# Keys and values of two groups by seven products in one bank; the value bias moved behind the context

## The chip, the cores and the metric

The kernel runs on one core of a Trainium2 chip. The metric is the device time of one launch in microseconds (us). An executed kernel has five engines beside its DMA queues: PE multiplies matrices into PSUM, the accumulators, which come in banks; DVE, ACT and POOL do the elementwise work (POOL on SBUF alone); SP issues most of the DMAs. PEld is PE's weight load, which runs beside its matmuls.

## The reference

One transformer layer in fp32, x of shape (2, 512, 512): grouped attention with 32 query heads and 8 key-value groups of width 128, then a layer norm, then a linear layer with low-rank experts and a router, then a layer norm. What matters here is the attention:

```
q = hidden_states @ Wq + bq
k = hidden_states @ Wk + bk
v = hidden_states @ Wv + bv
...
q = _rope(q, pos)
k = _rope(k, pos)
...
probs = jax.nn.softmax(scores, axis=-1)
ctx = jnp.einsum('bgrst,bgtd->bgrsd', probs, v)
...
return ctx @ Wo + bo
```

Causal scores are masked before the softmax, so each row of probs sums to one.

## The kernel before

**Units.** The work is cut into 16 units, one for each pair of group and batch row; the last two groups are taken with the batch outside. A unit has 16 slots, numbered through all units by T (256 in all, some 2.9 us each in the middle). One slot scores 32 query positions of four heads against the keys so far (`score`, L488), takes the masked maximum on DVE (L496), the exponential on ACT (L503), a reciprocal (L507), the normalisation on ACT (L511) and block transposes on DVE (L519, L521), each of these one or more slots behind. Four slots make a part; the probabilities go through DRAM to be transposed (L529, L537), and `weigh` (L544) multiplies them by the values twelve slots behind. `context_out` (L550) copies the result to SBUF on ACT.

**The order** is written out by hand: `slot(T)` issues in a fixed sequence what each engine does in that slot, and `put(T, f)` adds single steps (loads, sums of weights) to the end of a slot. Each engine takes its instructions in that order. What is issued for PE stands at the head of the slot: a product of queries, a product of keys or values, a product of the output, the score, the contexts.

**Seven products.** Queries and the output projection are multiplied as two-by-two block matrices by seven block products instead of eight. The sums of blocks of x are made once (`x_sums`), the sums of weight blocks on POOL (`strassen_sums`, L416 to L419), and the products of a pair of heads run through two PSUM tiles, qx and qy, in the order of `q_products` (two matmuls of 256 columns each, L429). Three times the running sum in qx is copied to small tiles by ACT and once to its place (`q_copy`, L457 and L460), and DVE adds qy to the three small ones (`q_sum`, L467, L470, L472).

**Keys** are made plainly, one unit ahead: four matmuls of 512 columns in slots 0 to 3 of a unit (`k_mm`, L355, tile pp, one PSUM bank that has the tag "k"), then the rotation in three steps on DVE from PSUM (L368, L371, L375) and a sum on POOL (L376).

**Values** are made plainly too, for two groups at a time: for a tile of 128 tokens, four matmuls of 256 columns with x as the weights (`v_mm`, L342, tile pv). In the middle of the kernel a unit makes two such tiles, in slots 7, 8, 11 and 12, in the same bank "k". DVE adds the bias, which is broadcast over all partitions by a DMA, and writes them to SBUF (`v_out`, L347), into one of eleven tiles. The first pair's eight tiles and three of the second pair's are made before or early in the slots, in other banks.

**Experts.** `lora_weights` transposes gathered rows on PE in three steps at slots 12, 14 and 16: the rows of the low-rank factors (L283), the router's rows (L289), and the other factors (L295). The bank tag is "wx".

Of the kernel before, what the change touches and what calls it, by code (L numbers as in the profile page):

```python
# [15 lines left out]
P = 128  # L16
H = 32
# [12 lines left out]
def postln_layer_kernel(  # L30
# [85 lines left out]
    bqkT = const.tile([P, H + G], F32, name="bqkT")  # L116
# [44 lines left out]
    def load_wv(gg):  # L161
        wv_g = wts.tile([P, KC, VN], F32, tag="wv_g", name=f"wv_{gg}", bufs=1)
        nc.sync.dma_start(out=wv_g, in_=Wv[:, ts(gg, VN)].rearrange("(c p) n -> p c n", p=P))
        bv_g = wts.tile([P, VN], F32, tag="bv_g", name=f"bv_{gg}")
        nc.sync.dma_start(out=bv_g, in_=bv[ts(gg, VN)].partition_broadcast(P))
        wvs[gg] = wv_g, bv_g
# [22 lines left out]
    bqk = setup.tile([H + G, D], F32, name="bqk")  # L189
    nc.scalar.dma_start(out=bqk[:H, :], in_=bq.rearrange("(h d) -> h d", d=D))  # L190
    nc.scalar.dma_start(out=bqk[H:, :], in_=bk.rearrange("(h d) -> h d", d=D))
# [27 lines left out]
    a_act = setup.tile([EAR, HID], F32, name="a_act")  # L219
    r_act = setup.tile([EA, HID], F32, name="r_act")  # L220
# [42 lines left out]
    def gather_experts():  # L263
        gather(a_act, lora_A.rearrange("e r n -> (e r) n"), idx["a"])
        gather(r_act, router_W, idx["e"])
# [72 lines left out]
    def v_mm(gg, t, c, pool, tag):  # L338

        if c == 0:  # L340
            psq["v", gg, t] = pool.tile([P, VN], F32, tag=tag, name="pv")
        nc.tensor.matmul(  # L342
            psq["v", gg, t], lhsT=xT[:, c, ts(t, P)], rhs=wvs[gg][0][:, c, :], start=(c == 0), stop=(c == KC - 1))
# [14 lines left out]
    def rope_step(key, bias_col, part, dst):  # L358
# [14 lines left out]
        else:  # L373
# [3 lines left out]
                dst, t1[:].rearrange("p (n s) -> p n s", s=BLK), t2[:].rearrange("p (n s) -> p n s", s=BLK), ALU.add)  # L377
# [76 lines left out]

    def q_copy(u, k, name):
        if name == "c21":
            nc.scalar.copy(psq["q", u, 2 * k + 1][:, :TH], halves[u, k]["qx"])  # L457
            return
        part = halves[u, k][name] = proj.tile([P, TH], F32, tag=name, name=name)
        nc.scalar.copy(part, halves[u, k]["qx"])  # L460

    def q_sum(u, k, step):
        key = u, k
        z = halves[key]
        if step == 0:
            psq["q", u, 2 * k] = proj.tile([P, S], F32, tag="raw0", name="q0", bufs=2)
            nc.vector.tensor_tensor(psq["q", u, 2 * k][:, :TH], z["qy"], z["p1"], ALU.add)  # L467
        elif step == 2:
            psq["q", u, 2 * k + 1] = proj.tile([P, S], F32, tag="raw1", name="q1")
            nc.vector.tensor_tensor(psq["q", u, 2 * k + 1][:, TH:], z["qy"], z["u3"], ALU.add)  # L470
        else:
            nc.vector.tensor_tensor(psq["q", u, 2 * k][:, TH:], z["qy"], z["u2"], ALU.add)  # L472
# [66 lines left out]
    def weigh(p, j):  # L539
        u, i = parts[p]  # L540
        g, b = unit(u)
        if j == 0:
            psc[p] = ps_ctx.tile([P, R, P], F32, tag="ctx", name="pc")
        nc.tensor.matmul(  # L544
            psc[p], lhsT=v_sb[g // VG, b * TPB + j][:, ts(g % VG, D)], rhs=pT[p][:, :, ts(j, P)],
# [591 lines left out]
```

## Time and profile before

| | |
|---|---|
| median of 4 runs | 841.21 us (840.48 to 846.49) |
| the profiled execution | 840.93 us |
| its span, first to last instruction | 839.1 us |
| mean granted clock of PE | 0.996 |
| weight loads and matmuls recorded | 3201 of each |
| key matmuls of 512 columns (L355, from wk) | 128 records |
| value matmuls of 256 columns (L342) | 256 records |
| value results with bias on DVE (L347) | 32, mean 410 ns |
| context copies on ACT (L550) | 64, mean 586 ns |
| value bias loads by SP | 4 of 128 KB, 6.7 us to landing |

The profile is of one execution. A group of instructions is named by its line, engine and operation, then "out<-in" by the program's tile names, then shapes, then the number of records; behind the bar stand busy time in us, the mean of one in ns, and the idle time of the engine before them with what ended it. Matmuls overlap, so the mean duration of one is longer than the distance from its start to the next; the modelled ends make a busy PE look fuller than it is. The start times of the timeline have no such trouble.

### The profile page before, as it was taken

How to read it: one execution, taken by the hardware profiler on the slowest of the kernel's cores; microseconds unless marked ns; L12 is line 12 of the kernel's file. 1: busy time of each engine (PE TensorE's matmuls, PEld its weight loads, DVE VectorE, ACT ScalarE, POOL GpSimd, SP SyncE). 2: the span in 40 equal slices, each digit the busy share in tenths (PEclk: the TensorE clock that was granted, in tenths of full speed). 3: DMA queues.
4: the chain of work that ended last, by engine and by line, in shares of the span. 5: the costliest groups of instructions: out<-in, count | busy, mean ns of one | idle time of the engine just before them, and what ended most of it. 6: DMA issues, size and time to landing. Idle time of an engine off the chain costs nothing.

```text
span 839.1 us, 10734 instructions
## 1 busy us (share of the span) xinstructions
PE 826.4 (98%) x3201; PEld 584.4 (70%) x3201; DVE 595.4 (71%) x1963; ACT 353.0 (42%) x1000; POOL 292.4 (35%) x319
## 2 busy tenths in 40 slices
PE   9999999999999999999999999999999999999996
PEld 5567767677777777777777777777777776555564
DVE  4468977787767876786867866787767968853534
ACT  1225454544435344434435344434434444662132
POOL 6463344233332334233332334344333523300023
PEclk9999999999999999999999999999999999999998
DMA  9126536463653556362653556273644545674211
GB/s 292 35 64 194 152 96 183 110 186 103 157 155 101 163 165 170 79 189 85 154 152 102 163 165 174 71 220 111 152 135 130 164 113 187 171 231 113 62 39 62
DMA packets 84971, 116.47 MB, mean 139 GB/s; under 512 B 6581, under 2 KB 64797, under 8 KB 82866
## 3 DMA queue, kind: packets, MB, share of 16 engines
q1 hardware_dynamic: 84258, 115.50, 48.4%
q0 software_dynamic: 448, 0.14, 0.2%
q8 instruction: 25, 0.41, 0.2%
q14 instruction: 32, 0.26, 0.1%
q10 hardware_dynamic: 208, 0.15, 0.1%
HBM read 71.73 MB, written 44.04 MB: 138 GB/s over the span
## 4 chain that ended last, share of the span: by engine, by line
PE 93%; DVE 4%; DMA 1%; ACT 1%; POOL 1%; issue 1%; SPq 0%; DVEq 0%; POOLq 0%
PE pc L544 16%; PE sc L488 13%; PE qx L429 11%; PE wx L429 11%; PE pp L355 10%; PE qy L429 8%; PE wy L429 8%; PE pv L342 7%; PE py L679 3%; PE po L615 3%; PE tp L274 1%; PE py L724 1%; DMA pT<-db 1%; DMA db<-zt 0%; DVE wt L568 0%
## 5 line engine op out<-in xcount | busy, mean ns | idle before, releaser
L503 ACT ACTIVATE p<-sc,nmax 128x288 f32<-128x288 f32 (+15 forms) x256 | 124.4, 486 | 253.1 <-DVE nmax L496 207.6
L496 DVE CUSTOM_DVE_ANT_0 sc<-sc,maskw 128x288 f32<-128x288 f32 (+15 forms) x256 | 114.2, 446 | 154.3 <-PE sc L488 151.6
L544 PE MATMUL pc<-pT,v 128*128 128x512 f32 x320 | 165.5, 599 | 0.4 <-DMA pT<-db 0.4
L488 PE MATMUL sc<-kT,qT 128*128 128x160 f32 (+15 forms) x512 | 162.0, 398 | 1.1 <-ACT p L503 1.1
L376 POOL TENSOR_TENSOR qT<-q,t 128x512 f32<-128x512 f32 x56 | 71.2, 1271 | 187.9 <-DVE q L375 187.9
L511 ACT ACTIVATE p<-p,den 128x288 f32<-128x288 f32 (+15 forms) x256 | 133.4, 522 | 0.1
L488 PEld LDWEIGHTS sc<-kT,qT 128*128 128x128 f32 x512 | 96.7, 190 | 30.3 <-issue 14.3
L416 POOL TENSOR_TENSOR cs<-ctxT 128x256 f32<-128x256 f32 x28 | 26.5, 947 | 196.1 <-PE wy L429 109.4
L550 ACT COPY ctxT<-pc 128x512 f32<-128x512 f32 x64 | 37.5, 586 | 124.0 <-PE pc L544 124.0
L519 DVE STREAM_TRANSPOSE zt<-p 128x128 f32<-128x128 f32 (+2 forms) x192 | 81.7, 426 | 0.0
L544 PEld LDWEIGHTS pc<-pT,v 128*128 128x128 f32 x320 | 57.0, 190 | 19.5 <-issue 5.4
L355 PE MATMUL pp<-xT,wk 128*128 128x512 f32 x128 | 65.0, 593 | 0.5 <-ACT xT L275 0.5
L342 PE MATMUL pv<-wv,xT 128*128 128x256 f32 x256 | 63.6, 379 | 0.0
L429 PE MATMUL wx<-wo,ctxT 128*128 128x256 f32 x224 | 57.7, 380 | 0.4 <-DVE den L507 0.4
L429 PE MATMUL qx<-xs,wq 128*128 128x256 f32 x224 | 58.0, 381 | 0.0
L342 PEld LDWEIGHTS pv<-wv,xT 128*128 128x128 f32 x256 | 48.5, 190 | 13.4 <-issue 6.9
L521 DVE STREAM_TRANSPOSE zt<-p 128x32 f32<-128x32 f32 (+3 forms) x256 | 57.5, 225 | 0.0
L429 PEld LDWEIGHTS qx<-xs,wq 128*128 128x128 f32 x224 | 41.4, 190 | 22.3 <-issue 16.0
L429 PEld LDWEIGHTS wx<-wo,ctxT 128*128 128x128 f32 x224 | 42.4, 190 | 13.5 <-issue 7.6
L503 ACT ACTIVATION_READ_ACCUMULATOR p<-sc,nmax 128x1 f32 x256 | 49.9, 195 | 0.0
L601 DVE TENSOR_TENSOR x_sb<-wx,x_sb 128x256 f32<-128x256 f32 x112 | 47.0, 419 | 0.0
L368 DVE SCALAR_TENSOR_TENSOR t<-q,bqkT,rope_sb 64x512 f32<-64x512 f32 x56 | 43.0, 768 | 1.3
(187 smaller groups left out, 1365.2 us busy)
## 6 DMA issues: line engine op xcount, KB each, us to landing
db<-zt SPq DMA_DIRECT2D x64, 256.0 KB, 4.2
pT<-db SPq DMA_DIRECT2D x16, 1024.0 KB, 4.8
db<-zt SPq DMA_DIRECT2D x64, 192.0 KB, 3.3
pT<-db SPq DMA_DIRECT2D x16, 768.0 KB, 4.4
wq<-in_L_attn_Wq_dram SPq DMA_DIRECT2D x20, 512.0 KB, 4.8
wo<-in_L_attn_Wo_dram SPq DMA_DIRECT2D x10, 1024.0 KB, 7.6
db<-zt SPq DMA_DIRECT2D x64, 128.0 KB, 2.4
pT<-db SPq DMA_DIRECT2D x16, 512.0 KB, 4.2
```

What stands on the lines that cost most here:

```text
L342: nc.tensor.matmul(psq["v", gg, t], lhsT=xT[:, c, ts(t, P)], rhs=wvs[gg][0][:, c, :], start=(c == 0), stop=(c == KC - 1))
L355: nc.tensor.matmul(psq[key], lhsT=wt[:, c, cols], rhs=xT[:, c, ts(b, S)], start=(c == 0), stop=(c == KC - 1))
L376: nc.gpsimd.tensor_tensor(dst, t1[:].rearrange("p (n s) -> p n s", s=BLK), t2[:].rearrange("p (n s) -> p n s", s=BLK), ALU.add)
L429: nc.tensor.matmul(ps, lhsT=wt[:, c, :], rhs=xt[:, c, :], start=start and c == 0, stop=c == CH - 1, skip_group_check=True)
L488: nc.tensor.matmul(sc[s][:, :w], lhsT=qT[u][:, i * QB + n].rearrange("p r s -> p (r s)"), rhs=kT[u][:].rearrange("p n s -> p (n s)")[:, :w ...
L496: nc.vector.tensor_tensor_reduce(sc[s][:, :w], sc[s][:, :w], maskw[:, S - w :], -SCALE, -MASKED, ALU.add, ALU.min, nmax[s])
L503: nc.scalar.activation(ptile[s][:, :w], sc[s][:, :w], AF.Exp, bias=nmax[s], scale=-1.0, accum_out=rden[s])
L511: nc.scalar.activation(ptile[s][:, :w], ptile[s][:, :w], AF.Copy, scale=rden[s])
L519: nc.vector.transpose(z[:, :, last - i : last, n, :].rearrange("p q j s -> p j q s"), ptile[s][:, : i * P])
L521: nc.vector.transpose(z[:, : n + 1, last, n, :], ptile[s][:, i * P : w])
L544: nc.tensor.matmul(psc[p], lhsT=v_sb[g // VG, b * TPB + j][:, ts(g % VG, D)], rhs=pT[p][:, :, ts(j, P)], start=(j == 0), stop=(j == i))
L601: nc.vector.tensor_tensor(into, pw[k, bank], into, ALU.add)
```

## The change

Units 0 to 3 keep their plain keys; the first pair of groups and half of the second keep plain values (pair 1's batch row 0, now four tiles). For all others, keys and values are made by seven block products for two groups and one batch row at a time: such a block takes a stretch of 16 slots, starting at slot 7 of a unit, with a product on every second slot and a result between them. Six blocks of keys and five of values fill the stretches one after another.

Both running sums of a block lie in the two halves of one bank. Four results a block are copied by ACT to the place in SBUF where the result belongs, and three are added there by DVE to what waits in that place. For keys the two blocks of columns are the two groups and the output is a unit's key tile, which is then rotated in place (key tiles: five instead of two). For values the weights of PE are blocks of x of 128 tokens, and the output has 128 columns.

The sums of weight blocks are made on POOL by the function that the queries use, six sets in all. The value bias is not added to the values: since the probabilities of a row sum to one, it is added to the context, by the instruction that copies it (now an activation with a bias of one column). It is loaded and transposed with the biases of queries and keys, and its four broadcast loads go. Plain value results become copies on ACT. The queries' partial results wait in the place of their result too, which takes away three small tiles. The router's rows are gathered into the tile of the low-rank rows and transposed with them. Loads of keys and values have other slots.

```
+    NBIAS = H + 2 * G
+    bqkT = const.tile([P, NBIAS], F32, name="bqkT")
...
-        bv_g = wts.tile([P, VN], F32, tag="bv_g", name=f"bv_{gg}")
-        nc.sync.dma_start(out=bv_g, in_=bv[ts(gg, VN)].partition_broadcast(P))
-        wvs[gg] = wv_g, bv_g
+        wvs[gg] = wv_g
...
-    bqk = setup.tile([H + G, D], F32, name="bqk")
+    bqk = setup.tile([NBIAS, D], F32, name="bqk")
     nc.scalar.dma_start(out=bqk[:H, :], in_=bq.rearrange("(h d) -> h d", d=D))
-    nc.scalar.dma_start(out=bqk[H:, :], in_=bk.rearrange("(h d) -> h d", d=D))
+    nc.scalar.dma_start(out=bqk[H : H + G, :], in_=bk.rearrange("(h d) -> h d", d=D))
+    nc.scalar.dma_start(out=bqk[H + G :, :], in_=bv.rearrange("(h d) -> h d", d=D))
     for t in range(TPB):
         load_x(t, 1)
...
-    a_act = setup.tile([EAR, HID], F32, name="a_act")
-    r_act = setup.tile([EA, HID], F32, name="r_act")
+    ar_act = setup.tile([EAR + EA, HID], F32, name="ar_act")
...
-        gather(a_act, lora_A.rearrange("e r n -> (e r) n"), idx["a"])
-        gather(r_act, router_W, idx["e"])
+        gather(ar_act[:EAR, :], lora_A.rearrange("e r n -> (e r) n"), idx["a"])
+        gather(ar_act[EAR:, :], router_W, idx["e"])
         for a in range(EA):
             gather(b_act[:, a, :], lora_B.rearrange("e (p j) r -> (e p) (j r)", j=BJ), idx["b"][:, a : a + 1])
...
-            ta = ps_wo.tile([P, KC, EAR], F32, tag="wx", name="ta")
+            ta = ps_wo.tile([P, KC, EAR + EA], F32, tag="wx", name="ta")
             for c in range(KC):
-                nc.tensor.transpose(ta[:, c, :], a_act[:, ts(c, P)], ident[:EAR, :EAR])
-            nc.vector.tensor_copy(arT[:, :, :EAR], ta)
+                nc.tensor.transpose(ta[:, c, :], ar_act[:, ts(c, P)], ident[: EAR + EA, : EAR + EA])
+            nc.vector.tensor_copy(arT, ta)
             nc.vector.tensor_copy(b_jar, b_act.rearrange("p a (j r) -> p j a r", r=RK))
-        elif step == 1:
-            tr = ps_wo.tile([P, KC, EA], F32, tag="wx", name="tr")
-            for c in range(KC):
-                nc.tensor.transpose(tr[:, c, :], r_act[:, ts(c, P)], ident[:EA, :EA])
-            nc.vector.tensor_copy(arT[:, :, EAR:], tr)
         else:
...
-            psq["v", gg, t], lhsT=xT[:, c, ts(t, P)], rhs=wvs[gg][0][:, c, :], start=(c == 0), stop=(c == KC - 1))
+            psq["v", gg, t], lhsT=xT[:, c, ts(t, P)], rhs=wvs[gg][:, c, :], start=(c == 0), stop=(c == KC - 1))
+    def v_of(gg, b):
+        if (gg, b) not in v_sb:
+            v_sb[gg, b] = work.tile([P, TPB, VN], F32, tag="v", name=f"v_{gg}_{b}", bufs=3)
+        return v_sb[gg, b]
     def v_out(gg, t):
-        v_sb[gg, t] = work.tile([P, VN], F32, tag="v", name=f"v_{gg}_{t}", bufs=11)
-        nc.vector.tensor_tensor(v_sb[gg, t], psq["v", gg, t], wvs[gg][1], ALU.add)
+        nc.scalar.copy(v_of(gg, t // TPB)[:, t % TPB, :], psq["v", gg, t])
     in_psum = set()
...
+    def k_of(u):
+        if u not in kT:
+            kT[u] = work.tile([P, UNIT, BLK], F32, tag="kT", name=f"kT_{u}", bufs=5)
+        return kT[u]
     def k_rope(u, part):
         if part == 0:
-            kT[u] = work.tile([P, UNIT, BLK], F32, tag="kT", name=f"kT_{u}")
+            k_of(u)
         rope_step(("k", u), H + unit(u)[0], part, kT[u])
...
+    def q_half(u, k, name):
+        head, half = {"p1": (0, 0), "u2": (0, 1), "c21": (1, 0), "u3": (1, 1)}[name]
+        return psq["q", u, 2 * k + head][:, half * TH : (half + 1) * TH]
     def q_copy(u, k, name):
-        if name == "c21":
-            nc.scalar.copy(psq["q", u, 2 * k + 1][:, :TH], halves[u, k]["qx"])
-            return
-        part = halves[u, k][name] = proj.tile([P, TH], F32, tag=name, name=name)
-        nc.scalar.copy(part, halves[u, k]["qx"])
-    def q_sum(u, k, step):
-        key = u, k
-        z = halves[key]
-        if step == 0:
+        if name == "p1":
             psq["q", u, 2 * k] = proj.tile([P, S], F32, tag="raw0", name="q0", bufs=2)
-            nc.vector.tensor_tensor(psq["q", u, 2 * k][:, :TH], z["qy"], z["p1"], ALU.add)
-        elif step == 2:
+        elif name == "u3":
             psq["q", u, 2 * k + 1] = proj.tile([P, S], F32, tag="raw1", name="q1")
-            nc.vector.tensor_tensor(psq["q", u, 2 * k + 1][:, TH:], z["qy"], z["u3"], ALU.add)
+        nc.scalar.copy(q_half(u, k, name), halves[u, k]["qx"])
+    def q_sum(u, k, name):
+        into = q_half(u, k, name)
+        nc.vector.tensor_tensor(into, halves[u, k]["qy"], into, ALU.add)
+    kvs = {}
+    KV_STEPS = {0: 1, 2: 2, 4: 6, 6: 7, 8: 4, 10: 5, 12: 3}
+    KV_OUT = {1: "p1", 3: "c11", 5: "u2", 7: "u3", 9: "c21", 11: "c22", 13: "c12"}
...
+    KV_ON_ACT = ("p1", "u2", "u3", "c21")
+    def kv_block(kind, p, h, c):
+        if kind == "k":
+            return wqk["k", VG * p + h][:, CH * c : CH * (c + 1), :]
+        return wvs[p][:, CH * c : CH * (c + 1), ts(h, D)]
+    def kv_sums(kind, p):
+        w = kvs[kind, p] = late["pool"].tile([P, 3, CH, D], F32, tag="kvs", name=f"kvs_{kind}_{p}")
+        strassen_sums(
+            nc.gpsimd, *(kv_block(kind, p, h, c) for h in range(2) for c in range(2)), *(w[:, m] for m in range(3)))
+    def kv_products(kind, p, b, step):
+        key = kind, p, b
+        x1, x2 = (xT[:, CH * c : CH * (c + 1), ts(b, S)] for c in range(2))
+        if step == 1:
+            halves[key] = ps_k.tile([P, 2, TH], F32, tag="k", name=f"{kind}x")
+        half, w, xt = {
+            1: (0, (0, 0), x1[:, :, :TH]), 2: (1, (0, 1), x2[:, :, :TH]), 6: (0, 1, xs[:, b, 1]),
+            7: (0, (1, 0), xs[:, b, 2]), 4: (0, (1, 1), xs[:, b, 3]), 5: (1, 0, xs[:, b, 0]),
+            3: (1, 2, x2[:, :, TH:]),
+        }[step]
+        w = kv_block(kind, p, *w) if isinstance(w, tuple) else kvs[kind, p][:, w]
+        ps = halves[key][:, half]
+        first = step in (1, 5)
+        if kind == "k":
+            product(ps, w, xt, first)
         else:
-            nc.vector.tensor_tensor(psq["q", u, 2 * k][:, TH:], z["qy"], z["u2"], ALU.add)
+            for t in range(2):
+                for c in range(CH):
+                    nc.tensor.matmul(
+                        ps[:, ts(t, P)], lhsT=xt[:, c, ts(t, P)], rhs=w[:, c, :],
+                        start=first and t == c == 0, stop=c == CH - 1, skip_group_check=True)
+    def kv_out(kind, p, b, name):
+        h, half = {
+            "p1": (0, 0), "c11": (0, 0), "u2": (0, 1), "c12": (0, 1), "c21": (1, 0), "u3": (1, 1), "c22": (1, 1)}[name]
+        x, y = (halves[kind, p, b][:, n] for n in range(2))
+        if kind == "k":
+            u = units.index((VG * p + h, b))
+            into = k_of(u)[:, half * (UNIT // 2) : (half + 1) * (UNIT // 2), :].rearrange("p n s -> p (n s)")
+            psq["k", u] = kT[u][:].rearrange("p n s -> p (n s)")
+        else:
+            into = v_of(p, b)[:, 2 * half : 2 * half + 2, ts(h, D)]
+            x, y = (z.rearrange("p (t d) -> p t d", d=D) for z in (x, y))
+        if name in KV_ON_ACT:
+            nc.scalar.copy(into, x)
+        else:
+            nc.vector.tensor_tensor(into, y, into, ALU.add)
     def q_rope(u, r, part):
         if u not in qT:
...
     def context_out(p):
         ctxT[p] = work.tile([P, R, P], F32, tag="ctxT", name=f"ctxT_{p}", bufs=3)
-        nc.scalar.copy(ctxT[p], psc[p])
+        col = H + G + unit(parts[p][0])[0]
+        nc.scalar.activation(ctxT[p], psc[p], AF.Identity, bias=bqkT[:, col : col + 1])
...
-    for n, gg, t in [(2 * t - 1, 0, TPB + t) for t in range(TPB)] + [(2 * t + 11, 1, t) for t in range(3)]:
+    for n, gg, t in [(2 * t - 1, 0, TPB + t) for t in range(TPB)] + [(2 * t + 11, 1, t) for t in range(TPB)]:
         put(n, lambda gg=gg, t=t: v_tile(gg, t, ps_wo, "wx"))
...
-        put(12 + 2 * k, lambda k=k: lora_weights(k))
+        if k < 2:
+            put(12 + 4 * k, lambda k=k: lora_weights(k))
     put(1, lambda: load_q(1, 1))
     put(6, lambda: load_wv(1))
...
-        put(2 * UNIT * (g - 1) - 24, lambda g=g: load_k(g))
-    for gg in range(2, G // VG):
-        put(4 * UNIT * (gg - 1) + 30, lambda gg=gg: load_wv(gg))
+    PLAIN_K = 2 * B
+    KV_FROM = 7
+    late = {}
+    PERIOD = VG * B * UNIT
+    for p in range(1, G // VG):
+        at = PERIOD * p
+        put(8 if p == 1 else at - PERIOD + 8, lambda p=p: load_k(VG * p))
+        put(36 if p == 1 else at - PERIOD + 10, lambda p=p: load_k(VG * p + 1))
+        put(40 if p == 1 else at - 2 * UNIT + 3, lambda p=p: kv_sums("k", p))
+        if p > 1:
+            put(at - PERIOD + 34, lambda p=p: load_wv(p))
+        put(at + (UNIT if p == 1 else 0) + 3, lambda p=p: kv_sums("v", p))
+    def kv_at(T):
+        frame, o = divmod(T - KV_FROM, UNIT)
+        p, k = divmod(frame + B, VG * B)
+        kind, b = "kv"[k // B], k % B
+        if 0 < p < G // VG and (kind, p, b) != ("v", 1, 0):
+            return (kind, p, b), o
+        return None, None
     def wo_from(u):
...
-        if 0 < uk < NU and l < KC:
+        if 0 < uk < PLAIN_K and l < KC:
             k_mm(uk, l)
-        gv, tv = divmod(2 * (uk - 3) + (l >= 11), NT)
-        gv += 1
-        new_v = 0 < gv < G // VG and (gv > 1 or tv >= 3)
-        if new_v and l in (7, 8, 11, 12):
-            for c in range(2):
-                v_mm(gv, tv, 2 * (l in (8, 12)) + c, ps_k, "k")
+        kv, o = kv_at(T)
+        if kv and o in KV_STEPS:
+            kv_products(*kv, KV_STEPS[o])
         kw, sw = divmod(T - LAG_WO, 8)
...
+        if kv and KV_OUT.get(o) in KV_ON_ACT:
+            kv_out(*kv, KV_OUT[o])
         for part, j in weigh_at.get(T - 1, ()):
...
-            q_sum(uq, kq, {1: 0, 5: 2, 7: 3}[step])
+            q_sum(uq, kq, {1: "p1", 5: "u3", 7: "u2"}[step])
+        if kv and o in KV_OUT and KV_OUT[o] not in KV_ON_ACT:
+            kv_out(*kv, KV_OUT[o])
         if 0 <= T - 2 < T_END:
             reciprocals(T - 2)
         if 0 <= T - 4 < T_END:
...
-        if new_v and l in (10, 14):
-            v_out(gv, tv)
         if plain and step_o:
             wo_out(p)
...
-    tb = ps_sc.tile([P, H + G], F32, tag="sc", name="tb")
-    nc.tensor.transpose(tb, bqk, ident[: H + G, : H + G])
+    tb = ps_sc.tile([P, NBIAS], F32, tag="sc", name="tb")
+    nc.tensor.transpose(tb, bqk, ident[:NBIAS, :NBIAS])
     nc.vector.tensor_copy(bqkT, tb)
     for c in range(KC):
...
+    late["pool"] = proj_stack.enter_context(tc.tile_pool(name="late", bufs=1))
     T_PROJ = T_END - 19
```

More of the change, by code (lines that the diff above doesn't have):

```diff
@@ L115, in postln_layer_kernel @@
     rope_sb = const.tile([P, 2, S], F32, name="rope_sb")
-    bqkT = const.tile([P, H + G], F32, name="bqkT")
+    NBIAS = H + 2 * G
+    bqkT = const.tile([P, NBIAS], F32, name="bqkT")
     OH, ARH = O // 2, EAR // 2
@@ L376, in rope_step @@
             nc.gpsimd.tensor_tensor(
-                dst, t1[:].rearrange("p (n s) -> p n s", s=BLK), t2[:].rearrange("p (n s) -> p n s", s=BLK), ALU.add)
+                dst, t1[:, :].rearrange("p (n s) -> p n s", s=BLK), t2[:, :].rearrange("p (n s) -> p n s", s=BLK), ALU.add)
     def k_mm(u, c):
@@ L544, in weigh @@
         nc.tensor.matmul(
-            psc[p], lhsT=v_sb[g // VG, b * TPB + j][:, ts(g % VG, D)], rhs=pT[p][:, :, ts(j, P)],
+            psc[p], lhsT=v_sb[g // VG, b][:, j, ts(g % VG, D)], rhs=pT[p][:, :, ts(j, P)],
             start=(j == 0), stop=(j == i))
@@ L807, in postln_layer_kernel @@
             put(q_from(set_units(before)[-1], k_before) + 8, lambda n=n, k=k: load_q(n, k))
-    for g in range(2, G):
-        put(2 * UNIT * (g - 1) - 24, lambda g=g: load_k(g))
-    for gg in range(2, G // VG):
-        put(4 * UNIT * (gg - 1) + 30, lambda gg=gg: load_wv(gg))
+    PLAIN_K = 2 * B
[17 more added lines that the diff above has]
+        return None, None
     def wo_from(u):
```

## The prediction

> **What bounds the kernel now.** I read first the totals at the head of the page (engine, busy us, share of the span, instructions):
>
> ```profile
> span 839.1 us, 10734 instructions
> ...
> PE 826.4 (98%) x3201; PEld 584.4 (70%) x3201; DVE 595.4 (71%) x1963; ACT 353.0 (42%) x1000; POOL 292.4 (35%) x319
> ...
> PE 93%; DVE 4%; DMA 1%; ACT 1%; POOL 1%; issue 1%; SPq 0%; DVEq 0%; POOLq 0%
> ```
>
> PE is busy for all but 12.7 us, and the chain that ended last (second line) is PE for 93%. The busy time by stretches says where the 12.7 us lie: 1.9 in the first 50 us, 0.3 from 50 to 100, none from 100 to 700, the rest in the tail. So in the long middle, where nearly all of the change lies, time is the sum of what PE streams. As PE's ends are modelled, I price by starts, from PE's timeline (start, length, operation, records merged):
>
> ```profile
> 11.54 7.03 PE L355 MATMUL pp<-xT,wq 128*128 128x512 f32 x16
> 18.41 1.89 PE L342 MATMUL pv<-wv,xT 128*128 128x256 f32 x8
> ...
> 29.21 5.34 PE L342 MATMUL pv<-wv,xT 128*128 128x256 f32 x24
> 34.39 6.17 PE L355 MATMUL pp<-xT,wq 128*128 128x512 f32 x14
> ```
>
> 16 records of 512 columns take 18.41 - 11.54 = 6.87 us, 0.4294 each; 24 of 256 take 5.18, 0.2158 each. A matmul of the program is two records, each with a weight load of its own. The same view later in the span has short ones:
>
> ```profile
> 308.91 0.30 PE L488 MATMUL sc<-kT,qT 128*128 128x32 f32 x2
> 309.05 1.10 PE L544 MATMUL pc<-pT,v 128*128 128x512 f32 x2
> 309.99 1.03 PE L429 MATMUL qx<-xs,ws 128*128 128x256 f32 x4
> ...
> 318.18 0.38 PE L488 MATMUL sc<-kT,qT 128*128 128x128 f32 x2
> 318.40 1.03 PE L429 MATMUL wy<-wo,cs 128*128 128x256 f32 x4
> ```
>
> Two records of 128 columns take 0.22 us, 0.110 each. Two of 32 and two of 512 take 309.99 - 308.91 = 1.08 us, of which the long two are 0.86: a record of 32 holds PE for 0.11, not the 0.027 of its columns. That is the weight load showing. At 128 columns load and stream just balance.
>
> **PE's work, part by part.** The groups by line and shape say how much there is:
>
> ```profile
> L355 PE MATMUL pp<-xT,wk 128*128 128x512 f32 x128 | 65.0, 593 | 0.5 <-ACT xT L275 0.5
> L342 PE MATMUL pv<-wv,xT 128*128 128x256 f32 x256 | 63.6, 379 | 0.0
> ```
>
> *Keys.* 128 records are 16 units of 4 matmuls. Units 0 to 3 stay; 12 units leave: 96 records x 0.4294 = 41.2 us. In come six (pair, batch) blocks of seven products, each two matmuls of 256 columns, so 28 records: 168 x 0.2158 = 36.3. **-5.0 us**.
>
> *Values.* 256 records are 32 tiles of 4 matmuls; 12 tiles stay (eight of pair 0, four of pair 1), 20 leave: 160 x 0.2158 = 34.5 us. In come five blocks of seven products, but with x as weights and 128 columns of output: four matmuls each, 56 records a block, 280 in all. At 0.110 that is 30.8: **-3.7 us**. Here one eighth of the arithmetic goes, yet the records rise from 160 to 280, each with a weight load: this is the step that could turn. Its price lies between 0.108 (half of 0.2158) and 0.190, the duration of one such load; I take 0.110, because the 128-column score is the same shape and type and its two loads are in that spacing.
>
> The Trainium skill speaks against this step ("TensorE: Matmul & The Clock Gate", Back-to-back issue gap): in a stream of load and matmul pairs it gives 81 ns a matmul of 128 columns against 56 for one alone. An estimate by that page's ratio, 1.45, makes 0.159 of my 0.110, and the values 10 us dearer instead of 3.7 cheaper. The trace's 0.22 us for two, loads included, decides for me.
>
> *Router.* Its four transposes (L289, 4 records, 0.4 us) become four more rows of L283's: **-0.3**, between 0 and -0.4.
>
> Sum: -9.0 us.
>
> **What lies beside PE.** ACT: 12 plain value copies and 44 of the blocks, 56 x 0.367 (L457, same shape) = 20.6; the bias makes L550 an activation, 0.687 (the 512-wide exponential, which reads a bias too) for 0.586, x64 = 6.5. ACT goes from 353 to 380 of 830. DVE: -32 x 0.41 (L347), +33 x 0.415 (L467's form): +0.6 of 595. POOL: six sums of four instructions, 0.731 + 0.907 + 0.763 + 0.753 = 3.15 us a set (rows of L416 to L419): +18.9 of 292. All three are hidden by PE's 817 us; uncovered they would matter only as lateness within a slot, which I follow for each queue:
>
> ACT. Behind a block's copy stand context copy, normalisation and exponential of that slot, and score needs the exponential of two slots before. Copies come on slots 8, 12, 14 and 0 of 16 and delay these by 0.37. The narrowest place is the 64-wide score (ACT's timeline):
>
> ```profile
> 313.91 0.59 ACT L550 COPY ctxT<-pc 128x512 f32<-128x512 f32 x1 [2.49 <-PE pc L544]
> ...
> 315.02 0.30 ACT L503 ACTIVATE p<-sc,nmax 128x64 f32<-128x64 f32 x1
> 315.21 0.20 ACT L503 ACTIVATION_READ_ACCUMULATOR p<-sc,nmax 128x1 f32 x1
> ```
>
> It is done at 315.41; the score that needs it, two slots on, starts at 318.18: 2.77 us to spare. The key products that stand between move to odd slots, and one group of 0.86 falls away here: 1.9 left. Cost 0.
>
> Bias: no row has this activation function. From below its end is 0; from above, a table change before and after it, 2 x 1.283 (ACT_TABLE_LOAD rows) + 0.1 = 2.67 in each of 64, which goes 0.8 past the 1.9 at 16 of them: +12 us. I take 0: L550's copies stand between exponentials with no load (two loads at L503 in 256).
>
> POOL. Block sums are issued three or four slots ahead of the product that needs them (over 8 us at about 2.9 a slot) for 3.15 us of work; behind them wait the context sums, due three slots later. Cost 0, or some tenths once.
>
> SP: key loads move earlier and in pairs, the value load four slots later; each still lands 30 slots ahead, the first pair's second key 4 slots (4.7 us to land, some 11 there). Four bias loads leave; a small one joins ACT's queue, in before PE's transpose at 7.3. Cost 0.
>
> DVE. A block's last value sum is issued two slots before the context that reads it, its last key sum twelve before the score. Key rotations now read SBUF where they read PSUM: 0.768, 0.748 and 0.710 in the rows of the queries, which do so, for 0.755, 0.744 and 0.730. Sums that wait in their place save three small tiles and add one wait (ACT's copy into the tile that DVE has just summed), a slot apart; by the exponentials' 1.9 us of spare time that is 0.
>
> Start. Twelve value results go from DVE (42.8 of 50 us busy from 50 to 100) to ACT (23.2): nothing, or up to the 0.6 us of idle that is not the wait for the first inputs. Pair 1's fourth tile is made at slot 17 in a bank that a DVE copy of 1.07 us (L296) has to leave: 0, at worst a stall like the one before 95.26 us (0.34, PE on DVE q L470) once.
>
> PE's new waits: each block product must wait until the other half of its bank has been read, in the slot before. Queued behind it is all of PE. For such a wait the trace has this (waiting, releaser, us in total, times, longest):
>
> ```profile
> PEld qy L429 <- DVE q L470: 4.9, 8, 1.2
> ...
> PE qy L429 <- DVE q L470: 0.3, 1, 0.3
> ```
>
> 28 sums of queries have the same one-slot distance; loads waited 4.9 us, PE itself 0.3. The block products stand behind the query products, 0.86 us later. From below 0, from above 4.9/28 = 0.175 at each of the 33 sums by DVE: 5.8. I take 0.
>
> **Rivals.**
> 1. *Forecast*, 80%: 840.93 (the profiled execution: span 839.1 and 1.8 around it) - 9.0 = **831.9**. The median shown, 841.21, is 0.03% above that execution; I leave the number. Its own range: 0.112 for the value record +0.6, 51 ns semaphore steps at the 35 value products +1.8, scatter and start +0.5: 834.8; start-up idle gone and scatter -1.6: 830.3.
> 2. *The bank is the new wait*, 8%: 831.9 + 5.8 = 837.7. For: one bank for both halves; against: 0.3 us of PE in 28.
> 3. *Slower: the weight load shows in the value products*. 5%. Place: 280 records; price 0.190 each is 53.2 us instead of 30.8: 854.3. It decides from (34.5 + 5.0 + 0.3)/280 = 0.142 us a record. For: loads last 0.190; against: the pair of 0.22.
> 4. *Table changes at the bias*, 3%: 831.9 + 12 = 844.
>
> The remaining 4% lies around them unnamed. The range 829.8 to 838.2 holds cases 1 and 2. A measurement of this kernel tells from no change what is over about 0.5% (4.2 us): faster 0.83 (case 1 and most of the rest below 837.0), same 0.09 (cases 2 and 4 in part), slower 0.08 (case 3, most of 4).
>
> **What would show it.** Right: 32 records at L355's keys and 96 at L342; 168 and 280 new ones at 0.216 and 0.110 from start to start; PE still without idle between 100 and 700 us; span near 830. Wrong: value records over 0.142 apart; PE idle, or loads late, released by a block's copy or sum; more than the present ACT_TABLE_LOADs; the exponential ending later than the score two slots on.

## The result and the profile after

The changed kernel takes 841.43 us (median of 44 runs, 837.97 to 846.92) where the kernel before, beside it, takes 841.88 (70 runs): a ratio of 0.9991, with a 95% interval of 0.9981 to 1.0. No difference can be measured; the forecast was 831.9. The runs of one kernel differ by some us, and they are longer where the mean granted clock of PE is lower (of the 44, the 14 at 0.996 or more have a median of 839.3 us, the 28 at 0.994 or less one of 842.6), so profiles are best compared at one clock. The profiled execution took 840.51 us at 0.996, as the one before did; its span is 838.4.

The head of the page, and the chain that ended last by engine (the lines before stand in the prediction):

```profile
span 838.4 us, 11168 instructions
...
PE 819.2 (98%) x3389; PEld 597.9 (71%) x3389; DVE 607.7 (72%) x1963; ACT 377.1 (45%) x1056; POOL 323.4 (39%) x343
...
PE 88%; DVE 6%; DMA 2%; ACT 1%; issue 1%; POOL 1%; SPq 0%; DVEq 0%; POOLq 0%
```

PE's busy time fell by 7.2 us, and the span by 0.7. The share of PE in the chain fell from 93% to 88%; DVE's rose from 4% to 6%, the DMAs' from 1% to 2%. So work went from PE as meant, and PE now waits. The matmuls first, by line and shape (columns as in the table of the time before):

```profile
L338 PE MATMUL pv<-wv,xT 128*128 128x256 f32 x96 | 22.4, 380 | 0.0
L355 PE MATMUL pp<-xT,wk 128*128 128x512 f32 x32 | 16.0, 596 | 0.5 <-ACT xT L276 0.5
L512 PE MATMUL vx<-wv,xs 128*128 128x128 f32 x80 | 10.5, 275 | 0.0
```

96 and 32 plain records are left, as forecast. The last row is one of four groups of block values, 280 records in all; block keys have 168 (L434, kx). Their price is read from PE's timeline, from start to start:

```profile
293.73 1.05 PE L512 MATMUL vx<-kvs_v,xs 128*128 128x128 f32 x8
294.62 1.03 PE L434 MATMUL wx<-wt,ctxT 128*128 128x256 f32 x4
```

Eight value records take 0.89 us, 0.111 each; four key records, read in the same way, take 0.86, 0.215 each. Over all of them, from start to start, that is 31.2 and 36.3 us, where the forecast had 30.8 and 36.3. So PE gained 34.5 - 31.2 = 3.3 us with the values, 41.2 - 36.3 = 4.9 with the keys (the forecast's 5.0, but for rounding) and, as forecast, some 0.3 with the router: 8.5 us. The list of waits (waiting, releaser, us in total, times, longest) says where it went; before, PE's product of queries did not stand in this list but once, with 0.3:

```profile
PE qy L434 <- DVE q L474: 4.2, 7, 0.6
...
PE pc L602 <- DMA pT<-db: 1.8, 1, 1.8
...
PEld qy L434 <- DVE q L474: 12.5, 14, 1.5
```

Seven times a product of queries waits for DVE's query sum (L474). Measured by starts, six of these delays are of 0.78 to 0.81 us and one of 0.55, 5.3 in all, and the records behind a late product lose another 0.1 each time. They come at seven of the eight places at which DVE begins to make the weight sums of the output (wt, L627): one in every 32 slots, and the last one 16 slots after. One delay of 2.0 us more is at the first context (72.83 us), which waits for a DMA.

One of the seven places, in both kernels' timelines, with the rows that matter of DVE, POOL and PE (L601 and L660 are sums for the output, L470 and L474 the query sum, L416 to L419 and L421 to L424 POOL's sums). Both come to it at the same time, 365.9 us. Before:

```profile
366.76 0.71 DVE L375 SCALAR_TENSOR_TENSOR q<-q,bqkT,rope_sb 128x512 f32<-128x512 f32 x1
366.90 1.16 POOL L416 TENSOR_TENSOR cs<-ctxT 128x256 f32<-128x256 f32 x1 [6.65 <-ACT p L503]
367.51 0.76 DVE L368 SCALAR_TENSOR_TENSOR t<-pp,bqkT,rope_sb 64x512 f32<-64x512 f32 x1
...
370.03 0.41 DVE L470 TENSOR_TENSOR q<-qy,u 128x256 f32<-128x256 f32 x1
370.63 1.03 PE L429 MATMUL qy<-xT,ws 128*128 128x256 f32 x4
```

After:

```profile
366.56 0.41 DVE L530 TENSOR_TENSOR kT<-kx,kT 128x256 f32<-128x256 f32 x1
366.91 0.73 POOL L421 TENSOR_TENSOR cs<-ctxT 128x256 f32<-128x256 f32 x1 [5.35 <-ACT p L561]
...
367.08 1.10 DVE L375 SCALAR_TENSOR_TENSOR q<-q,bqkT,rope_sb 128x512 f32<-128x512 f32 x1
...
368.22 1.10 DVE L368 SCALAR_TENSOR_TENSOR t<-kT,bqkT,rope_sb 64x512 f32<-64x512 f32 x1
...
370.96 0.41 DVE L474 TENSOR_TENSOR q<-qy,q 128x256 f32<-128x256 f32 x1
371.42 0.92 PE L434 MATMUL qy<-xT,ws 128*128 128x256 f32 x3 [0.65 <-DVE q L474]
```

Read DVE from top to bottom; left out are short instructions, a weight sum (1.14 us before, 1.12 after), a masked maximum and an output sum, the same in both. Before, the query sum is done at 370.44, and PE, which streams contexts until 370.63, never notices: 0.19 us to spare, of which the step from DVE's end to PE's start takes 0.05 (after the change, from 370.96 + 0.41 to 371.42). After, a sum of a key block (L530) stands in the queue, which costs 0.33; the query rotation behind it takes 1.10 instead of 0.71, and the key rotation 1.10 instead of 0.76; the weight sum gives back 0.12 from start to start. The query sum is issued 0.93 us later, and PE starts 0.79 later. The same is told by the groups of the key rotation, by its source, first before and then after:

```profile
L368 DVE SCALAR_TENSOR_TENSOR t<-pp,bqkT,rope_sb 64x512 f32<-64x512 f32 x24 | 18.0, 755 | 14.0 <-PE pp L355 13.5
```

```profile
L368 DVE SCALAR_TENSOR_TENSOR t<-kT,bqkT,rope_sb 64x512 f32<-64x512 f32 x12 | 13.2, 1101 | 0.4
```

From PSUM (pp) the instruction takes 0.755 us, also in the 12 that are left of it in the changed kernel; from SBUF (kT) it takes 1.10 at all twelve places, and at each of them one of POOL's sums had begun 0.50 to 0.63 us earlier.

### The profile page after: what moved, and what is told of

Same layout as the page of the kernel before. It is cut to its first block, busy times and chain, and to the rows that moved or that the text cites. A ratio compares the mean times of both kernels' runs of the same rounds, so it can differ in the third digit from the quotient of the medians.

```text
span 838.4 us, 11168 instructions
## 1 busy us (share of the span) xinstructions
PE 819.2 (98%) x3389; PEld 597.9 (71%) x3389; DVE 607.7 (72%) x1963; ACT 377.1 (45%) x1056; POOL 323.4 (39%) x343
## 4 chain that ended last, share of the span: by engine, by line
PE 88%; DVE 6%; DMA 2%; ACT 1%; issue 1%; POOL 1%; SPq 0%; DVEq 0%; POOLq 0%
PE pc L602 15%; PE sc L546 13%; PE qx L434 10%; PE wx L434 10%; PE qy L434 8%; PE wy L434 8%; PE pp L355 5%; PE kx L434 4%; PE vx L512 4%; PE py L738 3%; PE po L674 3%; PE pv L338 2%; DVE wt L627 1%; DVE t L368 1%; DVE q L375 1%; DMA pT<-db 1%
## 5 line engine op out<-in xcount | busy, mean ns | idle before, releaser
L376 POOL TENSOR_TENSOR qT<-q,t 128x512 f32<-128x512 f32 x56 | 73.3, 1309 | 178.9 <-DVE q L375 159.9
L609 ACT ACTIVATE ctxT<-pc,bqkT 128x512 f32<-128x512 f32 x64 | 44.0, 687 | 97.0 <-PE pc L602 97.0
L421 POOL TENSOR_TENSOR cs<-ctxT 128x256 f32<-128x256 f32 x28 | 25.6, 913 | 151.5 <-PE wy L434 107.3
L434 PE MATMUL wx<-wo,ctxT 128*128 128x256 f32 x224 | 57.7, 380 | 0.4 <-DVE den L565 0.4
L434 PE MATMUL qx<-xs,wq 128*128 128x256 f32 x224 | 58.0, 381 | 0.0
L434 PEld LDWEIGHTS qx<-xs,wq 128*128 128x128 f32 x224 | 41.4, 190 | 22.3 <-issue 18.7
L470 ACT COPY q<-qx 128x256 f32<-128x256 f32 x112 | 41.1, 367 | 18.2 <-PE qx L434 18.0
L368 DVE SCALAR_TENSOR_TENSOR t<-q,bqkT,rope_sb 64x512 f32<-64x512 f32 x56 | 46.9, 837 | 1.5
L660 DVE TENSOR_TENSOR x_sb<-wx,x_sb 128x256 f32<-128x256 f32 x112 | 47.0, 420 | 0.0
L434 PEld LDWEIGHTS wx<-wo,ctxT 128*128 128x128 f32 x224 | 41.2, 190 | 7.6 <-issue 1.9
L701 POOL TENSOR_SCALAR y<-y,mv_f,rstd_f 128x512 f32<-128x512 f32 x4 | 8.5, 2129 | 96.7 <-DVE rstd_f L698 72.0
L375 DVE SCALAR_TENSOR_TENSOR q<-q,bqkT,rope_sb 128x512 f32<-128x512 f32 x56 | 43.6, 779 | 0.0
```

The lines of the kernel that those rows point to most:

```text
L368: nc.vector.scalar_tensor_tensor(t2[lo, :], q[hi, :], b_ap[hi, :], rope_sb[hi, 1, :], ALU.add, ALU.mult)
L375: nc.vector.scalar_tensor_tensor(t1, q, b_ap, rope_sb[:, 0, :], ALU.add, ALU.mult)
L376: nc.gpsimd.tensor_tensor(dst, t1[:, :].rearrange("p (n s) -> p n s", s=BLK), t2[:, :].rearrange("p (n s) -> p n s", s=BLK), ALU.add)
L434: nc.tensor.matmul(ps, lhsT=wt[:, c, :], rhs=xt[:, c, :], start=start and c == 0, stop=c == CH - 1, skip_group_check=True)
L660: nc.vector.tensor_tensor(into, pw[k, bank], into, ALU.add)
```

## The experiments

**Theory A**: the block products are worth what was forecast, and DVE gives it back, because it is late at one query sum in 32 slots, by the added sum and by slower rotations. The main rival is that the block products themselves and their shared bank make PE wait (letter C in the first two runs, B in those with values alone and with one more sum; other runs have rivals of their own). The place is crowded because three things meet in the same four slots: the output weight sums on DVE (wt, L627, once in 32 slots), the key rotation (steps 4 to 6 of a unit) and POOL's context sums.

### Rotation later

```
-        if 0 < uk < NU and l in (KC, KC + 1, KC + 2):
-            k_rope(uk, l - KC)
+        turn = KC if uk < PLAIN_K or uk == NU - 1 else 11
+        if 0 < uk < NU and turn <= l < turn + 3:
+            k_rope(uk, l - turn)
```

> Theory A (DVE is late in slots 20 to 22 of every 32, where the block's last sum and the slower key rotation stand before the query sum that PE's product waits for): with the rotation of the block-made keys in steps 11 to 13 of a unit instead of 4 to 6, the seven waits of 0.55 to 0.81 us before that product go, some 5.5 us: about 835 us, ratio to before about 0.993. Rival B (PE itself comes earlier because the key products left slots 16 and 18, whatever DVE does): the waits stay, 840.5. Rival C (the waits are those of the shared bank): they stay, 840.5.

Measured: 835.17 us, a ratio of 0.9923 (0.9895 to 0.9951) to the kernel before. All products stay, three instructions a unit are moved by seven slots, and six of seven waits go; the one that is left (0.81 us, at 695.36) is that of the last unit, where the rotation was not moved:

```profile
PE qy L434 <- DVE q L474: 0.6, 1, 0.6
```

This is theory A's outcome: the products are worth their price once DVE is in time. Some 0.7 us of the gain are not the rotation's: the first context waits 1.3 us here instead of 2.0.

### Without the last sum of a block

```
-        else:
+        elif name != "c12":
             nc.vector.tensor_tensor(into, y, into, ALU.add)
```

> Leaves out the last of the seven results of each block (the sum by DVE that a quarter of keys and values needs; its product is still made). Theory A: DVE has 0.33 us less ahead of the query sum in six of the seven places; the waits fall from 0.8 to about 0.47 and stay 0.55 at the one place with no block: about 2 us less, 838.5. Rival B: no change in the waits, 840.5. Rival C: the waits change only if they stand at block products, which they do not: 840.5.

Measured: 837.13 us, 0.9941 (0.9918 to 0.9963). The waits go but for the one that has no block before it (0.55). One sum of 0.33 us thus decides over 0.8, more than its own length. The timeline shows why: the query rotation behind it starts 0.33 earlier, ahead of POOL's context sum, and takes 0.71 again.

```profile
364.67 0.71 DVE L375 SCALAR_TENSOR_TENSOR q<-q,bqkT,rope_sb 128x512 f32<-128x512 f32 x1
364.83 1.14 POOL L421 TENSOR_TENSOR cs<-ctxT 128x256 f32<-128x256 f32 x1 [5.35 <-ACT p L561]
```

Whichever of the two starts first keeps its speed here. The key rotation still takes 1.10, and alone it costs PE next to nothing: by starts 0.08.

### Without POOL's context sums

```
+        if k:
+            cs[k] = cs[0]
+            return
         c = cs[k] = work.tile([P, 3, CH, P], F32, tag="cs", name=f"cs_{k}", bufs=1)
-        strassen_sums(
-            nc.gpsimd, *(ctx_block(k, h, c_half) for h in range(2) for c_half in range(2)), *(c[:, n] for n in range(3)))
+        nc.gpsimd.memset(c, 0.0)
```

> Leaves out POOL's sums of the contexts (one tile of zeros in their place), so that POOL is quiet while DVE rotates keys and queries in slot 20. Theory A2 (the rotation from SBUF is slow because POOL works on SBUF beside it): the two DVE instructions of 1.10 us go back to 0.71 and 0.76, the waits shrink by 0.74 to about 0.1: 835.5. Rival D (reading keys from SBUF is slow as such): 1.10 stays, 840.5.

Measured: 839.01 us, 0.9966 (0.9948 to 0.9984), about half of what was expected. The same place in this kernel's timeline:

```profile
366.54 0.75 DVE L368 SCALAR_TENSOR_TENSOR t<-kT,bqkT,rope_sb 64x512 f32<-64x512 f32 x1
366.58 1.83 POOL L376 TENSOR_TENSOR qT<-q,t 128x512 f32<-128x512 f32 x1 [6.31 <-DVE q L375]
367.30 1.66 DVE L627 TENSOR_TENSOR wt<-wo 128x512 f32<-128x512 f32 x1
```

Both rotations are back, the query's at 0.71 (it starts at 365.79) and the key's at 0.75, as expected, although the key rotation reads SBUF: so it is POOL's work ahead of it that made it slow, not SBUF by itself. But POOL, with nothing to do, takes up its query sum earlier, and now the weight sum (L627) runs beside that and takes 1.66 instead of 1.12. Five of the waits shrink from 0.80 to 0.61 only, the last one to 0.74, and that at the place without a block grows from 0.55 to 0.75: 4.5 us in all instead of 5.3. In the profile the first context, with 0.9 instead of 2.0, has more part in the gain than they. The expectation had left out what POOL would do with its free time.

### Keys alone by seven products

```
+        if kv and kv[0] == "v":
+            if o % 2 == 0 and o < 16:
+                for c in range(2):
+                    v_mm(kv[1], TPB * kv[2] + o // 4, o % 4 + c, ps_k, "k")
-        if kv and o in KV_STEPS:
+        elif kv and o in KV_STEPS:
             kv_products(*kv, KV_STEPS[o])
```

(and `v_out` on each fourth slot of a stretch in place of `kv_out`, no sums of value weights, the value weights loaded five slots later)

> Values plain again in the same stretches of slots (four matmuls of 256 columns a tile, copied by ACT), keys by seven products. If the value products stream at 0.110 us a record as the profile of after has them, PE has eight groups of 0.863 instead of seven of 0.88 in five stretches, +3.7 us; DVE has no value sums, which shortens three of the seven waits by 0.33: about 843. If the value blocks gain nothing on PE: 840 or less.

Measured: 840.51 us, 0.9978 (0.9958 to 0.9998). Three of the waits, those at value blocks, go, and that at 277 us falls from 0.55 to 0.19; the three at key blocks stay at 0.8. The first context waits 0.4 instead of 2.0. The place at 277 us shows a second source of the waits: no block has a sum there, but in the changed kernel POOL's new sums of value weights (L424, wv) start 0.21 ahead of the query rotation and make it 1.07, and here these sums are gone. So the value products save 3.3 us of PE and gave back 3 x 0.8 + 0.36 of it in waits, and the difference of 1.6 at the first context, which no run ties to them, takes the rest: on balance they were worth nothing here. The 843 that was expected had left out both.

### Values alone by seven products

```
-        if kv and o in KV_STEPS:
+        if kv and kv[0] == "k":
+            if o in (0, 2, 6, 8):
+                u_kv = units.index((VG * kv[1] + o // 6, kv[2]))
+                for c in range(2):
+                    k_mm(u_kv, o % 6 + c)
+        elif kv and o in KV_STEPS:
             kv_products(*kv, KV_STEPS[o])
...
+            if o in (3, 9):
...
+                nc.scalar.copy(into, psq["k", u_kv])
```

> Values by seven products, keys plain again (four matmuls of 512 columns a unit, made in the same stretches, two copies by ScalarE into the SBUF tile; no block sums of keys on GpSimd, no sums of keys on VectorE). TensorE streams about 5.0 us more than in the changed kernel (168 records of 0.216 out, 96 of 0.429 in). Theory A (VectorE is late at the query sum): the three waits at key blocks lose the key sum's 0.33 but keep the slower rotation, so they go from 0.80 to about 0.5 (the 0.55 of the place without any block), the three at value blocks stay at 0.8: 841.4 + 5.0 - 0.9 = 845.5. Rival B (the shared bank of the key blocks is what TensorE waits for): the three waits vanish, 841.4 + 5.0 - 2.4 = 844.0. Rival C (the products are worth what TensorE streams and nothing else): 846.4.

Measured: 842.46 us, 1.002 (0.9995 to 1.0045), 3.0 below what A expected. The three waits at key blocks did not shrink to 0.5, they all but went, and the numbers alone would suit rival B better. The timeline decides, at the same place:

```profile
367.03 0.71 DVE L375 SCALAR_TENSOR_TENSOR q<-q,bqkT,rope_sb 128x512 f32<-128x512 f32 x1
367.08 1.25 POOL L421 TENSOR_TENSOR cs<-ctxT 128x256 f32<-128x256 f32 x1 [3.62 <-ACT p L561]
```

As in the run without the last sum, L375 gets in 0.05 us ahead of POOL and keeps its 0.71, so the missing sum takes away 0.33 + 0.39 at once: DVE's query sum starts at 370.51, and PE's product at 370.97, 0.18 after the context before it. B still needed a test of its own, the one before the last below.

### Rotation at steps 10 to 12, the last unit too

```
+        turn = KC if uk < PLAIN_K else 10
```

> All of the change, with the rotation of the keys made in blocks at steps 10 to 12 of every unit, the last one too, in place of 4 to 6. Theory A (rotation and output weight sums in the same four slots make VectorE late): the seventh wait, 0.81 us near 695 us, goes as the other six did with steps 11 to 13, and no new one comes: 835.2 - 0.8 = 834.4. Rival B: the last place has another cause or step 10 meets another busy slot: 835.2 or more, with a wait of the query product at a new place.

Measured: 835.83 us, 0.9919 (0.9896 to 0.9942); its profiled execution took 833.01. PE has no idle time between 100 and 700 us, and no query product waits. But in the last unit another instruction is now late:

```profile
PE wy L434 <- DVE x_sb L660: 1.6, 2, 1.2
```

```profile
709.42 1.22 DVE L375 SCALAR_TENSOR_TENSOR kT<-kT,bqkT,rope_sb 128x512 f32<-128x512 f32 x1
...
711.54 0.70 PE L434 MATMUL wy<-wo,ctxT 128*128 128x256 f32 x2 [1.24 <-DVE x_sb L660]
```

At these slots the key rotation falls on a query rotation (L375 after L375, the query's at 708.79), and the output sum behind both is late. For the six places A holds; in the last unit the wait moved on, to an output product, which is nearer to rival B's case.

### The same with small loads at the start

```
+        bv_g = wts.tile([P, 16], F32, tag="bv_g", name=f"bv_{gg}")
+        nc.sync.dma_start(out=bv_g, in_=bv[gg * VN : gg * VN + 16].partition_broadcast(P))
```

> As the run with the rotation at steps 10 to 12, with one small load (16 numbers to each partition, read by nobody) after each value load on SyncE's queue, where the kernel before had its bias loads. It tests the first context's wait at about 72 us (0.4 to 2.0 us in the changed kernels, none before). Theory S (the place of SyncE's instructions against the fetch of its code makes one issue 1.3 to 2.0 us instead of 0.54): that issue is back at about 0.5 us, the wait goes, 833.4 or a little more. Rival T (something else makes the issue long): the wait stays at 0.4 to 2.0 and the time is that of the run beside it.

Measured: 836.17 us, 0.992 (0.99 to 0.994), that of the run beside it. SP's issue of the probabilities (db) at this place, before and after the change:

```profile
62.33 0.54 SPq L529 DMA_DIRECT2D db<-zt  x1
```

```profile
62.78 1.68 SPq L587 DMA_DIRECT2D db<-zt  x1
```

In this run it takes 1.56 us. The long issue stays, and the first context waits 1.2 us. Theory S falls as it was tested: the absence of the bias loads is not the cause. What makes this issue long in all the changed kernels (1.3 to 2.0 us) stays open. The context waits 0.4 to 2.0 us in them, and not in step with the issue: with keys alone an issue of 1.79 us goes with a wait of 0.4, in the changed kernel one of 1.68 with 2.0. What differs is the load of the probabilities behind it (pT): issued at 65.99 and 65.90 us, it landed 5.2 and 6.9 us later; before the change it was issued at 64.27 and landed 5.9 later, 0.2 ahead of its context. Why the landings differ is open too.

### The kernel before with one more sum

```
+        if T % 32 == 20 and 32 < T < 230:
+            nc.vector.tensor_tensor(spent, maskw[:, : 2 * P], maskw[:, : 2 * P], ALU.add)
         if 0 <= T - 2 < T_END:
             reciprocals(T - 2)
```

> The kernel before, all products as they were, with one sum of 128x256 that nobody reads put on VectorE's queue in six slots (the 20th of each 32, from 52 to 212), where the changed kernel has a block's last sum. Theory A (VectorE has 0.19 us to spare before the query sum of the next slot): the sum puts 0.33 on the queue, and the query rotation behind it then starts after GpSimd's context sums and takes 1.10 instead of 0.71; key rotations read PSUM and stay at 0.76. So 0.33 + 0.39 - 0.19 = 0.53 us of wait of TensorE at the query product, six times: 3.2 us over the kernel before. Without the effect on the rotation: 0.14 each, 0.8 in all. Rival B (the waits come from the block products and their shared bank): 2 us of work on an engine that is busy 71% cost nothing, no new wait.

Measured: 844.42 us, 1.0048 (1.0026 to 1.0069): slower by 4.0 us, with 2.2 to 5.8 as the interval's ends (the medians lie 1.7 apart), where A gave 3.2 and B nothing. The profile has six new waits of 0.57 us by starts (A: 0.53), 3.4 in all, beside the one of before:

```profile
PE qy L429 <- DVE q L470: 2.8, 7, 0.4
```

```profile
367.31 0.42 DVE L893 TENSOR_TENSOR spent<-maskw 128x256 f32<-128x256 f32 x1
367.63 0.73 POOL L416 TENSOR_TENSOR cs<-ctxT 128x256 f32<-128x256 f32 x1 [6.65 <-ACT p L503]
367.84 1.07 DVE L375 SCALAR_TENSOR_TENSOR q<-q,bqkT,rope_sb 128x512 f32<-128x512 f32 x1
...
371.93 0.92 PE L429 MATMUL qy<-xT,ws 128*128 128x256 f32 x3 [0.40 <-DVE q L470]
```

There is no block product and no shared bank in this kernel. The sum pushes L375 behind POOL's start (1.07 instead of 0.71), L368, next on DVE, reads PSUM and stays at 0.76, and PE waits. The shared bank falls, and the two halves of A are seen apart: here the sum and the query rotation behind it, in the changed kernel the key rotation as well, in the run without the last sum the key rotation alone.

### The last unit at steps 7 to 9

```
+        turn = KC if uk < PLAIN_K else 11 if uk < NU - 1 else 7
```

> All of the change, rotation of block-made keys at steps 11 to 13, in the last unit at 7 to 9 (at 4 to 6 it left a wait of 0.81 us, at 10 to 12 waits of 1.2 and 0.4 of the output products). Theory A: at 7 to 9 it lies between the output weight sums and the dense results of the last unit, and both waits go: no wait of query products at all, 834.4. Rival B: every place in the last unit costs about as much, VectorE being full there: 835.2.

Measured: 835.17 us, 0.9919 (0.9894 to 0.9944), as with the rotation later. No query product waits. By starts, PE's delays of over 0.25 us in the last unit come to 0.47 + 0.61 + 0.31 = 1.4 us, against 2.2 with the rotation at steps 4 to 6, 1.9 at 10 to 12, and 1.2 in the kernel before. So the 0.8 that A gave is there in the profile; in the time it is too small to be seen, and the medians of the two kernels are the same.

## Why the prediction was wrong

**The step that failed** is "DVE", in the part on what lies beside PE. It asked of the added sums only when their own readers need them ("a block's last value sum is issued two slots before the context that reads it, its last key sum twelve before the score"), and not who waits for what is queued behind them. Behind them stands the query sum of the next slot, for which PE waits, and there DVE had 0.19 us to spare at the fullest of the 32 slots. The forecast's share of DVE, 71%, was a mean over slots of which only one counts. The sum (+0.33 us), the query rotation behind it (+0.39) and the key rotation (+0.34), less 0.12 at the weight sum, put the query sum back by 0.93 and made PE some 0.8 late at six places. At the seventh, without a block, it was 0.55, by POOL's new sums of value weights and the key rotation; the step "POOL ... Cost 0, or some tenths once" had asked only when POOL's own results are due.

**"Key rotations now read SBUF where they read PSUM"**, which the sum took at no cost, is the other half of it. The rows of the queries that stood for the price (0.768, 0.748, 0.710) are means: of the 56 behind the first, 53 took 0.75 us and three 1.08 to 1.10. At the place of the key rotation POOL is at its sums, and 0.755 became 1.101. The price taken was that of another neighbourhood.

**PE's own terms were right.** Keys 4.9 (forecast 5.0, the same but for rounding), values 3.3 (3.7: a record took 0.111, not 0.110). The estimate of 0.159 a value record by the Trainium skill ("TensorE: Matmul & The Clock Gate", Back-to-back issue gap) is not borne out: with its load, a record took 0.111.

**The sum** then is: -8.5 from the matmuls, +4.8 for the seven waits less the one of before, +0.7 for the slower records behind them, +2.1 at the first context, -0.6 at a late context that waited for a DMA before (733.75 us) and no longer does, +0.4 at the arrival of the inputs: -1.1; the span fell by 0.7. With the rotation moved, the ratio is 0.992, which makes 834.2 of the 840.93 that the forecast started from, 2.3 us above the forecast. The profiled executions at the same granted clock, 0.996, are a closer measure: with the rotation at steps 10 to 12 the span is 831.1 against 839.1 before, 8.0 of the 9.0 that were forecast (this execution is the fastest of its six; with the last unit at steps 7 to 9 it is 831.5, at 0.997). By starts, 0.5 us of the lacking 1.0 lie at the first context, 0.4 in the value records, 0.3 at the inputs, 0.1 in the last unit and behind it and 0.2 spread over the middle, and 0.5 was gained back by the one query wait of before (95.26 us).

**ACT** was right: 377.1 us busy (380 forecast). The context copy with its bias takes 0.687 us in 64 records (L609), and PE's score waits for ACT 1.3 us in all, 1.1 before; the table changes of rival 4 did not come.

**The rivals.** The shared bank (2) was named with nearly the right number, 5.8 (the waits came to 5.3), but by luck and for the wrong place: it took the wait of qy on DVE as a model for the block products, and the wait then came at qy itself. No block product stands in the list of waits. The weight load (3) and the tables (4) did not come. The start was allowed up to 0.6 lost; the first context lost 2.0, and that was not seen: SP's queue was followed by its loads alone, and not by how long an issue takes or when the first probabilities come back, which in the changed kernel were asked for 1.6 us later and took 1.0 longer. The cause of both is open.

**What the sign list caught:** "PE idle ... released by a block's copy or sum" was near it, but the releaser is a query sum, one place behind.

## What to carry to other kernels

A busy share does not say whether an engine has time: take the period of the schedule (32 slots here), go to its fullest slot, and count from there to the first instruction that the bound engine waits for; every instruction put ahead of that one comes off its spare time, whatever its own deadline is. When an operand moves from PSUM to SBUF, look at who else reads SBUF at that moment. And if a change brings nothing though its main term is right, look for one queue that is late at one place: here moving three instructions a unit by seven slots gave back 0.7% of the time.

## What the runs showed of the hardware

A rotation step on DVE with two tensors in SBUF (L368, L371, L375) took 0.70 to 0.76 us in 160 of its 204 records in the changed kernel and 0.91 to 1.80 in the other 44; with one of the two in PSUM it took 0.754 to 0.757 whether POOL was at work or not (12 rows of L368). In the rows shown, the one that started second paid: POOL's sum of 0.73 took 1.16, 1.14 and 1.25 where DVE was ahead of it by 0.14, 0.16 and 0.05 us, and DVE paid where POOL was ahead by 0.17 and 0.21. At starts 0.04 us apart or less the records do not tell who pays: in the run without the context sums DVE was 0.04 ahead twice, and paid nothing at 366.54 us and 1.1 us at 695.53. The Trainium skill has this rule ("SBUF — State Buffer", Who interferes with whom): a VectorE instruction with two inputs in SBUF contends with a GpSimd instruction that reads SBUF, one with at most one such input does not, and the order of issue says which is blocked. The trace agrees. The page has the second one blocked until the first is done, which would make an estimate of 0.56 + 0.71 = 1.27 us of the rotation that started 0.17 behind a POOL sum of 0.73; measured were 1.10. The difference is regular: in 43 of the 44 slow records DVE lost what was left of POOL's record when DVE began, less 0.16 us (L375) or 0.19 to 0.20 (L368, L371), and where 0.21 or less was left it lost next to nothing (0.02 at most). That suits a full block, if POOL lets go so much ahead of the end that its record shows; POOL's spans are rough, and no run here shows the moment itself.

Taking POOL's work away did not take the contention away: its next instruction came earlier and hit another neighbour (1.66 us at L627 for 1.12).
